# First layer of a graph network: for 66 blocks, one tile of rows is formed on TensorE instead of gathered; x waits in DRAM between the layers

## The chip, the core and the metric

The kernel runs on one core of a Trainium2 chip. The metric is the device time of one execution in microseconds (us); lower is better. A core has five engines with an instruction queue each: TensorE (PE in the profile; its weight loads are shown as PEld), VectorE (DVE), ScalarE (ACT), GpSimd (POOL) and SyncE (SP, which here only issues DMAs). TensorE writes its results to PSUM, a small accumulator memory of eight banks; the other working memory is SBUF.

## The reference

A graph of 6250 nodes with 128 features and 200,000 edges, sorted by destination. Two layers, each with a layer norm and a ReLU in front and the input added back:

```python
h = relu(layernorm(x))                      # layer 1: attention, 8 heads of 16
z = (h @ W).reshape(N, 8, 16)
el, er = einsum(z, attn_l), einsum(z, attn_r)
e = leaky_relu(el[src] + er[dst], 0.2)
a = exp(e - segment_max(e, dst)[dst])
out = segment_sum(z[src] * a, dst) / segment_sum(a, dst) + bias
x = x + out
h = relu(layernorm(x))                      # layer 2: messages with edge attributes
s, v = (h[:, :32] @ W_up_s), (h[:, 32:] by W_up_v)
tpw = silu(silu(edge_attr_8 @ A1 + b1) @ A2 + b2) @ A3
message = segment_sum(products of s[src], v[src], edge_attr_4, tpw, dst) / 10
x = x + (message by W_out_s, W_out_v)
```

Each layer thus needs, for each edge, the row of a table of nodes that `src` names: 136 numbers in layer 1 (128 features and 8 values of `el`), 128 in layer 2.

## The kernel before

Edges go in tiles of 128 (one edge to a partition): 1563 tiles. Sixteen tiles make a block, 98 blocks; the kernel first checks that the destinations of a block lie in a window of 128 nodes that moves on by 64 from block to block, and then runs `even_edges`.

**Set-up.** `tile_even_edges` computes the table of layer 1 (`t0`, in DRAM, `ft` in the profile) and starts the gathers of block 0 into `z_first`.

**Gathers.** `gather` (L830) issues one indirect DMA for each tile from GpSimd (L832): 128 indices from a column of `src_col` (`fsrc`), 128 rows of the table into one of the 16 columns of a tile `g`. `z_pool` holds five such tiles. `take_rows(g + 3)` is called at the head of iteration g of the block loop; GpSimd runs ahead of it as far as free `g` tiles allow, since nothing else is in its queue.

**Layer 1.** The loop `for g in range(NG - 3)` (L1288) is software pipelined and written out by hand, PE, DVE and ACT in the order of the text: iteration g does `logits` and `maxima` for block g, `neighbours`, `weights`, `weighted` and `sums` for block g - 1, and the destination side (`masks_of`, `turned`, `er_of`, `er_sum`) for block g + 1, and makes 0/1 matrices from the destinations (`ends_of`, which calls `one_hot`, L1043) for block g + 2. `logits` (L1112) is the first to read the gathered rows of block g: it starts an iteration. `sums` (L1171) is the weighted sum over the edges as matmuls, 16 tiles of float32, each as two matmul instructions, and the last reader of a `g` tile. `ended` adds up the windows; after every second block `node_x` to `node_s` do what follows for 128 nodes: x plus bias from `with_bias` (L1175), the sums divided, added to x, layer norm, `wup`, and the rows of the table of layer 2 (`t1`, also `ft` in the profile) to DRAM. x stays in `x_all` (`fx_all`), 25 KB in each partition of SBUF, from there to the end of layer 2. In PSUM the node step has a bank `p_n`, the others are `p_u`, `p_m`, `p_d` (two), `p_er` and `pe` (two).

**Layer 2.** The same gathers of 128 numbers from `t1`, a small network for each edge on TensorE (`network`, `tensor_weights`), products on VectorE (`messages`, L1458 to L1467), sums on TensorE (`sums1`, L1475), and `node1`, which adds to `x_all` and stores.

Of the kernel before, what the change touches and what calls it, by code (L numbers as in the profile page):

```python
# [9 lines left out]
F32 = mybir.dt.float32  # L10
BF = mybir.dt.bfloat16
I32 = mybir.dt.int32
AF = mybir.ActivationFunctionType
OP = mybir.AluOpType
# [4 lines left out]
P = 128  # L19
# [3 lines left out]
ZW = F + H  # L23
# [6 lines left out]
KB = 16  # L30
# [933 lines left out]
def even_edges(tc, v):  # L964
# [7 lines left out]
    with ExitStack() as ctx:  # L972
        const = ctx.enter_context(tc.tile_pool(name="fconst", bufs=1))
        z_pool = ctx.enter_context(tc.tile_pool(name="fz", bufs=5))

        def gathered(table, tiles, width):
            return gather(z_pool.tile([P, KB, ZW], F32, name="g"), table, tiles, width)
# [4 lines left out]
        nc.sync.dma_start(jp, nums[:, NB * KB + TG + P :])  # L982
        rsel = const.tile([P, P // KB, P], BF, name="frsel")
        nc.sync.dma_start(rsel, v["rsel"])
        x_all = const.tile([P, NX, P], F32, name="fx_all")
        bias_b = const.tile([P, F], F32, name="fbias_b")
        nc.sync.dma_start(bias_b, bias.to_broadcast([P, F]))
        wup = const.tile([P, P], F32, name="fwup")
# [70 lines left out]
            return carry, agg  # L1059


        in_order = {mybir.EngineType.PE, mybir.EngineType.DVE, mybir.EngineType.Activation}
        with tc.manual_schedule(engines=in_order), \
                tc.tile_pool(name="l0", bufs=2) as l0, \
                tc.tile_pool(name="l0n", bufs=2) as l0n, \
                tc.tile_pool(name="l0_ps", bufs=1, space=PSUM) as l0_ps:


            def ends_of(c, q):
# [103 lines left out]


            def with_bias(i, n):  # L1175
                x_i = x_all[:, i : i + n, :]
                nc.sync.dma_start(x_i, xp[i * P : (i + n) * P].rearrange("(j p) f -> p j f", p=P))
                nc.vector.tensor_add(x_i, x_i, bias_b[:, None, :].to_broadcast([P, n, F]))

            def node_x(u):  # L1180
                i, n, agg = u["i"], u["n"], u["agg"]
                x_i = x_all[:, i : i + n, :]
                if n == 1:
                    with_bias(i, n)
                rd = l0n.tile([P, 2, H], F32, name="rd")[:, :n]
                nc.vector.tensor_scalar(rd, agg[:, :n, F:ZW], 1e-9, None, op0=OP.max)
                nc.vector.reciprocal(rd, rd)
                sums_ = agg[:, :n, :F]
                heads = sums_.rearrange("p j (h d) -> p j h d", d=D)
                nc.vector.tensor_mul(heads, heads, rd.unsqueeze(3).to_broadcast([P, n, H, D]))  # L1190
                nc.vector.tensor_add(x_i, x_i, sums_)
                u["mv"] = moments(l0n, x_i, n, f"n{n}")

            def node_d(u):
# [2 lines left out]
            def node_h(u):  # L1197
                i, n = u["i"], u["n"]
                rs, mr = normal(l0n, u["mv"], u["rs"], n, f"n{n}")
                xn = u["xn"] = l0n.tile([P, 2, P], F32, name="xn")  # L1200
                nc.scalar.activation(xn[:, 0, :], x_all[:, i, :], AF.Identity, bias=mr[:, 0, :],
                                     scale=rs[:, 0, :])
                if n == 2:
                    nc.vector.tensor_scalar(xn[:, 1, :], x_all[:, i + 1, :], u["mv"][:, 1, 0:1],
                                            rs[:, 1, :], op0=OP.subtract, op1=OP.mult)

            def node_t(u):
                n = u["n"]
                p_n = l0_ps.tile([P, 512], F32, name="p_n")
                p_n = u["p_n"] = p_n.rearrange("p (j f) -> p j f", f=P)  # L1210
                for j in range(n):
                    nc.tensor.transpose(p_n[:, j, :], u["xn"][:, j, :], ident)
                h_t = u["h_t"] = l0n.tile([P, 2, P], F32, name="h_t")
                nc.scalar.activation(h_t[:, :n], p_n[:, :n], AF.Relu)

            def node_s(u):
                i, n, p_n = u["i"], u["n"], u["p_n"]
                for j in range(n):
                    nc.tensor.matmul(p_n[:, 2 + j, :], u["h_t"][:, j, :], wup, start=True, stop=True)
                sv = l0n.tile([P, 2, P], F32, name="sv")  # L1220
                nc.scalar.activation(sv[:, :n], p_n[:, 2 : 2 + n], AF.Copy, scale=PRE)
                first = i * P - W0
                if i == 0:
                    nc.sync.dma_start(t1[: P - W0, :], sv[W0:, 0, :])
                else:
                    nc.sync.dma_start(t1[first : first + n * P].rearrange("(j p) f -> p j f", p=P),
                                      sv[:, :n])
# [13 lines left out]
            def take_rows(g):  # L1241
                if 0 < g < NG:
                    c = cs[g]
                    t = c["b"] * KB + c["o"]
                    c["z"] = gathered(t0, range(t, t + c["kt"]), ZW)

            def bank_of(c, bank="p_u"):
                if c["o"] == 0:
# [39 lines left out]
            for g in range(NG - 3):  # L1288
                take_rows(g + 3)
                c, b4 = cs[g], (cs[g - 1] if g else None)  # L1290
                n1 = cs[g + 1] if g + 1 < NG else none
                n2 = cs[g + 2] if g + 2 < NG else none
                nodes = []
                logits(c)
                ends_of(n2, 0)
                if n1 is not none:
                    masks_of(n1)
                turned(n1, 0)
                maxima(c)
                ends_of(n2, 1)  # L1300
                if b4:
                    neighbours(b4, cs[g - 2] if g > 1 else None, c)
                    if g > 1:
                        nodes = ended(cs[g - 2], st)
                turned(n1, 1)
                er_of(n1, 0)
                if b4:
                    weights(b4)
                for n in nodes:
                    node_x(n)  # L1310
                er_of(n1, 1)
                turned(n1, 2)
                if b4:
                    bank_of(b4)
                    weighted(b4, 0)
                turned(n1, 3)
                er_of(n1, 2)
                if b4:
                    weighted(b4, 8)
                for n in nodes:  # L1320
                    node_d(n)
                    node_h(n)
                ends_of(n2, 2)
                er_of(n1, 3)
                if b4:
                    sums(b4, 0)
                for n in nodes:
                    node_t(n)
                if n1 is not none:
                    er_sum(n1)  # L1330
                ends_of(n2, 3)
                for n in nodes:
                    node_s(n)
                if b4:
                    sums(b4, 8)
                if g == NG - 4:
                    for q in range(4):
                        ends_of(c1, q)
                    masks_of(c1)
                    for q in range(4):  # L1340
                        turned(c1, q)
                        er_of(c1, q)
                    er_sum(c1)
            with_bias(NX - 2, 2)

            logits(c3)
            masks_of(c2)
# [49 lines left out]
        with tc.manual_schedule(engines=in_order), \  # L1397
# [72 lines left out]
            def sums1(u):  # L1470
# [3 lines left out]
                for k in range(m):  # L1474
                    nc.tensor.matmul(blk[b]["p_u"][:, :MW], u["s"][:, k, :], u["mj"][:, k, :],  # L1475
                                     start=k0 + k == 0, stop=k0 + k == KT[b] - 1)

            def node1(i, agg):
                x_i = x_all[:, i, :]
                p_n = l1_ps.tile([P, 4, P], F32, name="p_n", bufs=1)  # L1480
                for q in range(2):
                    nc.tensor.transpose(p_n[:, q, :], agg[:, q * P : (q + 1) * P], ident)
                m_t = l1n.tile([P, 2, P], F32, name="m_t")
                nc.scalar.copy(m_t, p_n[:, :2])
                for q in range(2):
                    nc.tensor.matmul(p_n[:, 2, :], m_t[:, q, :], wout[:, q, :], start=q == 0, stop=q == 1)
                nc.vector.scalar_tensor_tensor(x_i, p_n[:, 2, :], POST, x_i, op0=OP.mult, op1=OP.add)
                if i == 0:
                    nc.sync.dma_start(out[: P - W0, :], x_all[W0:, 0, :])
                else:  # L1490
                    nc.sync.dma_start(out[i * P - W0 : (i + 1) * P - W0, :], x_i)

# [18 lines left out]
                network(0, step)  # L1511
            tensor_weights(us[0])
            us[0]["s"] = one_hot(0, us[0]["m"], iota_p)
            ready, done = [], []
            carry = agg = None
            ends = None
            for i, u in enumerate(us):
                b, k0, m = u["b"], u["k0"], u["m"]
                if k0 == 0:
                    take_rows(b + 2)  # L1520
                if b + 1 < NB:
                    network(b + 1, k0 // 4)
                if i + 1 < NU:
# [32 lines left out]
            for j in range(2):  # L1556
                for q in range(2):
                    nc.tensor.matmul(p_o[:, j, :], m_t[:, 2 * j + q, :], wout[:, q, :],  # L1558
                                     start=q == 0, stop=q == 1)
            x_i = x_all[:, NX - 2 :, :]  # L1560
            nc.vector.scalar_tensor_tensor(x_i, p_o[:, :2], POST, x_i, op0=OP.mult, op1=OP.add)  # L1561
            nc.sync.dma_start(out[first:].rearrange("(j p) f -> p j f", p=P), x_i)

# [137 lines left out]
```

## Time and profile before

| | |
|---|---|
| time, median of 3 runs | 5254.23 us (5251.97 to 5270.86) |
| the profiled execution's own time | 4015.26 us |
| its span | 4013.5 us |
| granted TensorE clock, mean | 0.809 |
| layer 1, roughly | 93 to 2045 us of the span |
| layer 2, roughly | 2045 to 4008 us |

The profiled execution is 1239 us shorter than the median of the timed runs. No view of the profile shows what the timed runs have more.

The busy share of an engine is that of its instructions over the span; issuing a DMA from SP and waiting are not counted. In the second part of the page the span is cut into 40 slices, and a digit is a share in tenths; PEclk is the clock that the chip granted TensorE in tenths of the full one. In a row of a group of instructions stand the line, the engine, the operation, output and input, how often, the busy us and the mean ns of one, and after the second bar the idle time of the engine just before them and what ended it ("issue": nothing that the profile shows). The stretches give, for each, its length and the busy time of PE, PEld, DVE, ACT and POOL, each with its number of instructions, then the granted clock, the share of the DMA engines and GB/s.

### The profile page before, as it was taken

How to read it: one execution, taken by the hardware profiler on the slowest of the kernel's cores; microseconds unless marked ns; L12 is line 12 of the kernel's file. 1: busy time of each engine (PE TensorE's matmuls, PEld its weight loads, DVE VectorE, ACT ScalarE, POOL GpSimd, SP SyncE). 2: the span in 40 equal slices, each digit the busy share in tenths (PEclk: the TensorE clock that was granted, in tenths of full speed). 3: DMA queues.
4: the chain of work that ended last, by engine and by line, in shares of the span. 5: the costliest groups of instructions: out<-in, count | busy, mean ns of one | idle time of the engine just before them, and what ended most of it. 6: DMA issues, size and time to landing. Idle time of an engine off the chain costs nothing. (4 is left out here: it accounts for less than half of the span.)

```text
span 4013.5 us, 45637 instructions
## 1 busy us (share of the span) xinstructions
PE 2837.4 (71%) x14592; PEld 2369.6 (59%) x14592; DVE 2191.8 (55%) x5376; ACT 1374.3 (34%) x3450; POOL 2993.5 (75%) x3158
## 2 busy tenths in 40 slices
PE   3666666666666666666677777777787777787787
PEld 3665655565556555555665665565666555666565
DVE  4544444444444444444456666666666666666666
ACT  3322222222222222222333434344434343443443
POOL 6777777777777777777757777777777777777776
PEclk6666666666666666666679999999999999999999
DMA  7222222222222222222212222222222222222221
GB/s 206 57 57 58 57 58 57 58 57 58 57 58 57 58 58 58 57 58 57 58 48 60 60 59 61 59 60 59 60 60 60 59 61 59 60 59 60 60 60 51
DMA packets 174105, 248.25 MB, mean 62 GB/s; under 512 B 70944, under 2 KB 123072, under 8 KB 173856
## 3 DMA queue, kind: packets, MB, share of 16 engines
q0 software_dynamic: 100032, 211.47, 19.7%
q1 hardware_dynamic: 73536, 33.70, 3.1%
q8 instruction: 118, 1.93, 0.2%
q14 instruction: 131, 1.07, 0.1%
q10 hardware_dynamic: 288, 0.07, 0.0%
HBM read 234.73 MB, written 9.99 MB: 61 GB/s over the span
## 5 line engine op out<-in xcount | busy, mean ns | idle before, releaser
L832 POOL DMA_INDIRECT g<-ft,fsrc x3110 | 2959.7, 952 | 975.4 <-issue 892.3
L1475 PE MATMUL p_u<-mj,s 128*128 128x256 f32 x3126 | 802.8, 401 | 354.7 <-DVE mj L1467 354.0
L1475 PEld LDWEIGHTS p_u<-mj,s 128*128 128x128 f32 x3126 | 582.8, 195 | 547.3 <-DVE mj L1467 478.2
L1171 PE MATMUL p_u<-g,s 128*128 128x136 f32 x3062 | 581.8, 369 | 0.5 <-DVE g L1166 0.5
L1171 PEld LDWEIGHTS p_u<-g,s 128*128 128x128 f32 x3062 | 557.2, 273 | 0.6 <-DVE g L1166 0.6
L1458 DVE TENSOR_TENSOR vy<-g,p_i 128x384 f32<-128x384 f32 x391 | 216.5, 554 | 596.3 <-DMA g<-ft,fsrc 569.3
L1442 ACT ACTIVATE p_w<-p_w,yb 128x64 f32<-128x64 f32 x1563 | 450.3, 288 | 113.6 <-PE p_w L1438 73.5
L1112 DVE TENSOR_TENSOR e_s<-g,er 128x128 f32<-128x128 f32 (+1 forms) x98 | 28.4, 290 | 749.3 <-DMA g<-ft,fsrc 749.2
L1438 PE MATMUL p_w<-fa3p,h 128*128 128x256 f32 x1564 | 403.8, 381 | 0.0
L1088 PE MATMUL p_d<-fident,s 128*128 128x128 f32 x1563 | 392.8, 418 | 5.1 <-DVE s L1043 5.1
L1116 PE MATMUL pe<-fident,e_s 128*128 128x128 f32 x98 | 39.7, 406 | 454.0 <-DVE e_s L1113 454.0
L1438 PEld LDWEIGHTS p_w<-fa3p,h 128*128 128x128 f32 x1564 | 285.7, 193 | 120.9 <-issue 57.4
L1081 ACT COPY mk<-p_m 128x385 f32<-128x385 f32 (+1 forms) x99 | 47.6, 481 | 903.1 <-PE p_m L1078 903.1
L1088 PEld LDWEIGHTS p_d<-fident,s 128*128 128x128 f32 x1563 | 318.9, 229 | 43.6 <-DVE s L1043 31.6
L1423 ACT ACTIVATE h<-p_h,fb 128x512 f32<-128x512 f32 x196 | 134.7, 687 | 561.9 <-PE p_h L1421 561.9
L1090 ACT CAST d<-p_d 128x512 bf16<-128x512 f32 x391 | 228.5, 585 | 201.3 <-PE p_d L1088 153.5
L1166 DVE TENSOR_TENSOR g<-g,pe 128x1024 f32<-128x1024 f32 x193 | 225.4, 1208 | 127.8 <-ACT g L1157 125.2
L1116 PEld LDWEIGHTS pe<-fident,e_s 128*128 128x128 f32 x98 | 16.6, 169 | 470.6 <-issue 462.6
L1043 DVE TENSOR_TENSOR s<-p_i,fdloc 128x512 f32<-128x512 f32 x391 | 266.2, 681 | 14.5 <-ACT p_i L1417 14.5
L1043 DVE TENSOR_TENSOR s<-fiota,fdloc 128x512 f32<-128x512 f32 x391 | 265.6, 681 | 5.9 <-ACT fmasks L1036 5.8
L1428 ACT ACTIVATE h<-p_h,fb 128x512 f32<-128x512 f32 x196 | 134.7, 687 | 362.0 <-PE p_h L1425 362.0
L1462 DVE TENSOR_REDUCE vd<-vy 128x128 f32<-128x384 f32 x391 | 228.9, 585 | 0.0
(172 smaller groups left out, 3417.5 us busy)
## 6 DMA issues: line engine op xcount, KB each, us to landing
g<-ft,fsrc POOLq DMA_INDIRECT x3110, 2.5
ft<-in_e_f_dram SPq DMA_DIRECT2D x98, 64.0 KB
yb<-in_e_y_dram SPq DMA_DIRECT2D x98, 32.0 KB
fx_all<-in_e_xp_dram SPq DMA_DIRECT2D x48, 64.0 KB
ft<-sv SPq DMA_DIRECT2D x47, 64.0 KB
out_dram<-fx_all SPq DMA_DIRECT2D x47, 64.0 KB
ft<-zt SPq DMA_DIRECT2D x6, 408.0 KB
fxs<-in_e_xp_dram SPq DMA_DIRECT2D x6, 384.0 KB
```

Of the source, the lines that this page charges most:

```text
L832: nc.gpsimd.indirect_dma_start(out=to[:, k, :width], out_offset=None, in_=table, in_offset=bass.IndirectOffsetOnAxis(ap=src_col[:, t : t + ...
L1043: nc.vector.tensor_tensor(s[:, :m], iota[:, None, :].to_broadcast([P, m, P]), dloc[:, t : t + m].unsqueeze(2).to_broadcast([P, m, P]), OP. ...
L1088: nc.tensor.transpose(p_d[:, k, :], c["s"][q][:, k, :], ident)
L1090: nc.scalar.copy(d[:, :m], p_d[:, :m])
L1166: nc.vector.tensor_mul(zh, zh, p_a[:, k0 : k0 + m].unsqueeze(3).to_broadcast([P, m, H, D]))
L1171: nc.tensor.matmul(c["p_u"][:, :ZW], c["s"][k // 4][:, k % 4, :], c["z"][:, k, :], start=c["o"] + k == 0, stop=c["o"] + k == KT[c["b"]] - 1)
L1423: nc.scalar.activation(c["h1"], p_h, AF.Silu, bias=b1)
L1438: nc.tensor.matmul(w[:, k : k + n].rearrange("p k a u -> p (k a u)"), c["h2"][q // 4][:, q % 4, :], a3p[:, :n].rearrange("p k f -> p (k f) ...
L1442: nc.scalar.activation(w[:, k, ::2, :], w[:, k, ::2, :], AF.Copy, scale=c["yb"][:, k0 + k, 0:1])
L1458: nc.vector.tensor_mul(vy, v_n, y_p)
L1462: nc.vector.tensor_reduce(vd, vy.rearrange("p t i u -> p t u i"), AX.X, OP.add)
L1475: nc.tensor.matmul(blk[b]["p_u"][:, :MW], u["s"][:, k, :], u["mj"][:, k, :], start=k0 + k == 0, stop=k0 + k == KT[b] - 1)
```

## The change

In 66 blocks of layer 1 (`dense`: blocks 6 to 93 but those divisible by four) the sixteenth tile is no longer gathered. Its 128 rows come from TensorE as 0/1 matrix times table. The table, 50 tiles of 128 nodes, is held in SBUF as three bfloat16 parts that add up to the float32 value (`t0s`, 40 KB in each partition); `split` reads it back from DRAM, three tiles at a time, five times in each of the iterations 0 to 2 and twice in iteration 3. The 50 tiles are treated as three thirds of 17, 17 and 16. For a dense block `spread` turns the 128 source numbers (less their third's start) by one float32 matmul into a row that every partition holds, in the free quarter of the bank `pe`; `ends_to` compares it with the node numbers of each of the 17 positions (two VectorE instructions of 1152 and 1024 elements, output bfloat16, into the memory of `z_first`, which is free by then); `rows_of` multiplies each of the 17 0/1 matrices with the three parts of the up to three tiles at that position at once: 51 matmuls of 408 (three of them 272) columns, summed in the bank `p_n`; `taken` selects the third that the edge's source is in and writes column 15 of the `g` tile. The 51 matmuls of block b are put at six places in the iterations b - 2 (27 of them) and b - 1 (24). The node step gives up `p_n` and uses the end of `p_u`.

To make room `x_all` goes: `node_x` takes x in a tile of its own and stores it to a DRAM tile `x1`; layer 2 reads it back for each 128 nodes (`node_rows`) when their first block starts.

```diff
+        x1 = dram.tile([NX, P, P], F32, name="fx1")
-        x_all = const.tile([P, NX, P], F32, name="fx_all")
+        NR = -(-NX // 3)
+        dense = {b for b in range(6, NB - 4) if b % 4}
...
+            ND = NB - 1
+            key = l0d.tile([P, ND], F32, name="key")
+            nc.vector.tensor_scalar(key, src_col[:, KB - 1 : ND * KB : KB], float(W0), None, op0=OP.add)
+            part = l0d.tile([P, ND, 3], F32, name="part")
...
+            order = sorted(range(NR), key=lambda k: (k > 0, 2 * NR + k < NX, k))
+            half = (NR + 1) // 2
+            place = l0d.tile([P, NR], F32, name="place")
+            for j, k in enumerate(order):
+                nc.vector.tensor_scalar(place[:, j : j + 1], jp[:, 0:1], -1.0, float(P * k),
+                                        op0=OP.mult, op1=OP.add)
+            t0s = l0d.tile([P, 3, NX, ZW], BF, name="t0s")
+            def split(i, n):
+                zr = l0.tile([P, 3, ZW], F32, name="zr")[:, :n]
...
+                    nc.sync.dma_start(zr, rest.rearrange("(j p) f -> p j f", p=P))
+                r = l0.tile([P, 3, ZW], F32, name="zr2")[:, :n]
+                nc.scalar.copy(t0s[:, 0, i : i + n, :], zr)
+                nc.vector.tensor_sub(r, zr, t0s[:, 0, i : i + n, :])
+                nc.scalar.copy(t0s[:, 1, i : i + n, :], r)
+                nc.vector.tensor_sub(t0s[:, 2, i : i + n, :], r, t0s[:, 1, i : i + n, :])
+            def spread(c):
+                b = c["b"]
+                nc.tensor.matmul(c["at"]["pe"][:, 3 * P :], key[:, b : b + 1].to_broadcast([P, P]), ident,
+                                 start=True, stop=True)
+            def ends_to(c, h):
+                n = half if h == 0 else NR - half
+                oh = c["oh", h] = ohs[:, h * half : (h + 1) * half, :]
+                nc.vector.tensor_tensor(
+                    oh[:, :n], c["at"]["pe"][:, 3 * P :].unsqueeze(1).to_broadcast([P, n, P]),
+                    place[:, h * half : h * half + n].unsqueeze(2).to_broadcast([P, n, P]), OP.is_equal)
+            def rows_of(c, k0, n):
+                if k0 == 0:
+                    p_x = l0_ps.tile([P, 512], F32, name="p_n")
+                    c["p_x"] = p_x[:, : 3 * ZW].rearrange("p (r f) -> p r f", f=ZW)
+                for k in range(k0, min(k0 + n, NR)):
+                    i = order[k]
+                    m = len(range(i, NX, NR))
+                    for s in range(3):
+                        nc.tensor.matmul(c["p_x"][:, :m, :], c["oh", k // half][:, k % half, :],
+                                         t0s[:, s, i::NR, :], start=k == 0 and s == 0,
+                                         stop=k == NR - 1 and s == 2)
+            def taken(c):
+                b, z = c["b"], c["z"][:, KB - 1, :]
+                nc.vector.tensor_scalar(z, c["p_x"][:, 0, :], part[:, b, 0:1], None, op0=OP.mult)
+                for r in (1, 2):
+                    nc.vector.scalar_tensor_tensor(z, c["p_x"][:, r, :], part[:, b, r : r + 1], z,
+                                                   op0=OP.mult, op1=OP.add)
             def with_bias(i, n):
-                x_i = x_all[:, i : i + n, :]
+                x_i = l0n.tile([P, n, P], F32, name=f"x{n}", bufs=3 - n)
...
             def node_x(u):
                 nc.vector.tensor_add(x_i, x_i, sums_)
+                nc.sync.dma_start(x1[i : i + n].rearrange("j p f -> p j f"), x_i)
...
             def node_t(u):
-                p_n = l0_ps.tile([P, 512], F32, name="p_n")
+                if "bank" in u:
+                    p_n = u["bank"][:, 2 * P :]
...
             def take_rows(g):
-                    c["z"] = gathered(t0, range(t, t + c["kt"]), ZW)
+                    c["z"] = gathered(t0, range(t, t + c["kt"] - (c["b"] in dense)), ZW)
...
                 logits(c)
+                if to: spread(n2)
                 ends_of(n2, 0); masks_of(n1); turned(n1, 0); maxima(c)
+                if to: ends_to(n2, 0)
+                if at: rows_of(n1, half, 4)
                 ends_of(n2, 1); neighbours(b4, ...); turned(n1, 1); er_of(n1, 0)
+                if at: rows_of(n1, half + 4, NR)
                 weights(b4)
+                if at: taken(n1)
                 node_x; er_of(n1, 1); turned(n1, 2); weighted(b4, 0)
+                if to: ends_to(n2, 1)
                 turned(n1, 3); er_of(n1, 2); weighted(b4, 8)
+                if to: rows_of(n2, 0, 3)
                 node_d, node_h; ends_of(n2, 2); er_of(n1, 3); sums(b4, 0)
-                node_t
+                if to: rows_of(n2, 3, 3)
                 er_sum(n1); ends_of(n2, 3)
-                node_s; sums(b4, 8)
+                sums(b4, 8); node_t
+                if to: rows_of(n2, 6, half - 6)
+                node_s
+                for i in range(g * 15, min(g * 15 + 15, NX), 3):
+                    split(i, min(3, NX - i))
...
+            def node_rows(i, n=1):
+                x_i = l1n.tile([P, n, P], F32, name=f"x{n}", bufs=3 if n == 1 else 1)
+                nc.sync.dma_start(x_i, x1[i : i + n].rearrange("j p f -> p j f"))
+                return x_i
...
                 if k0 == 0:
                     take_rows(b + 2)
+                    if b % 2 == 0:
+                        xs[b // 2] = node_rows(b // 2, 1 if b < NB - 2 else 2)
```

The loop of layer 1 stands here shortened, several calls to a line (`to`: block g + 2 is dense; `at`: block g + 1 is); the lines with a plus are new, and `node_t` and `node_s` have moved behind the second half of `sums`.

## The prediction

> **What bounds the kernel now.** I read the page first, for the engine that never rests.
>
> ```profile
> PE 2837.4 (71%) x14592; PEld 2369.6 (59%) x14592; DVE 2191.8 (55%) x5376; ACT 1374.3 (34%) x3450; POOL 2993.5 (75%) x3158
> ...
> POOL 6777777777777777777757777777777777777776
> PEclk6666666666666666666679999999999999999999
> ...
> L832 POOL DMA_INDIRECT g<-ft,fsrc x3110 | 2959.7, 952 | 975.4 <-issue 892.3
> ```
>
> 75% does not look like a bound, but the row of the gathers shows what the other 25% are: 0.3 us of "issue" before each, a wait for nothing. So I took the groups of the even middle of layer 1 (200 to 2000 us of the span).
>
> ```profile
> L832 POOL DMA_INDIRECT g<-ft,fsrc x1426 | 1365.6, 958 | 434.6 <-issue 405.9 <-PE p_u L1171 11.3 <-DMA g<-ft,fsrc 8.2
> ...
> L1112 DVE TENSOR_TENSOR e_s<-g,er 128x128 f32<-128x128 f32 x89 | 26.0, 292 | 719.5 <-DMA g<-ft,fsrc 719.5
> ```
>
> A gather costs (1365.6 + 434.6) / 1426 = **1.262 us** of GpSimd, and 3126 of them 3945 of the 4013.5 us. The second row says the same from the other side: VectorE waits for the rows at the head of every block, 719.5 / 89 = 8.1 us. In the order of time one block starts at 996.48 and the next at 1016.74: 20.2 us, 16 gathers. The other waits of GpSimd are one of 27.9 us between the layers and pieces of 0.3 us.
>
> The engine that gets the work is TensorE, and its clock decides what it can take. These are the order of time on PE, twice the same 16 matmuls in one block, and stretches of 1 us in the block before.
>
> ```profile
> 1025.75 3.97 PE L1171 MATMUL p_u<-g,s 128*128 128x136 f32 x16
> ...
> 1030.52 2.02 PE L1171 MATMUL p_u<-g,s 128*128 128x136 f32 x16
> ```
>
> ```profile
> 1006.00:1007.00 1.00, 0.43 (x10) 0.33 (x9) 1.00 (x2) 0.58 (x1) 0.69 (x2) 0.50 0.10 26
> ...
> 1012.00:1013.00 1.00, 1.00 (x9) 1.00 (x8) 0.00 (x0) 0.00 (x0) 0.69 (x2) 0.73 0.17 44
> 1013.00:1014.00 1.00, 0.60 (x6) 0.40 (x4) 0.00 (x0) 0.00 (x0) 0.73 (x1) 1.00 0.27 70
> ...
> 1016.00:1017.00 1.00, 0.00 (x0) 0.00 (x0) 0.27 (x1) 0.00 (x0) 0.70 (x2) 0.50 0.11 30
> ```
>
> The clock is 0.50 or 1.00, nothing between: it rises after about 5.5 us without a gap (1006.9 to 1012.4) and falls after about 2.4 us of rest. In layer 2, where PE pauses for 1.3 us at most places, it stays at 1.00. The 0.6 of the page is a mean of the two. What a block costs at the full clock stands at the start of layer 1, where PE was late and worked through:
>
> ```profile
> 116.64 0.27 PE L1116 MATMUL pe<-fident,e_s 128*128 128x128 f32 x1
> 116.75 0.33 PE L1078 MATMUL p_m<-fmasks,frsel 128*128 128x385 bf16 x1
> ...
> 122.30 3.95 PE L1171 MATMUL p_u<-g,s 128*128 128x136 f32 x32
> ...
> 128.75 0.53 PE L1078 MATMUL p_m<-fmasks,frsel 128*128 128x385 bf16 x1
> ```
>
> From 116.64 to 126.25 is **9.6 us**, waits included, against 17.1 us (996.48 to 1013.60) for the same work mostly at half clock.
>
> **What goes.** 66 gathers x 1.262 = 83.3 us of GpSimd. Next in line is TensorE. Three dense blocks and one other take GpSimd 61 x 1.262 = 77.0 us, against 80.8 before.
>
> **What PE gets.** No row has a bf16 matmul of 408 columns in a stream. The nearest is the one of 385 columns above: 0.53 us at half clock, 0.33 at full, so the part that goes with the clock is 0.20 us at full clock, 0.21 for 408 columns. From below, page "TensorE: Matmul & The Clock Gate" of the Trainium skill (Part 2, Back-to-back issue gap) prices a stream at N/2.4 ns, an estimate of 0.17 us; float32 rows fit it (256 columns in 0.236 us, 8 in 1.89 us at 3000.97, at two passes each). I take 0.20: 51 x 0.20 = 10.2 us, and 0.2 for `spread` (four passes like it, L1088, took 0.60 us warm for four instructions, it has two). The node step adds some 0.5 us every second block. Four blocks: 4 x 9.9 + 3 x 10.4 = **70.8 us, 6.2 below GpSimd's 77.0** (66.3 at 0.17, 72.3 at 0.21). It is a little better than that, since the 9.6 us hold 2 us of waits for ACT and the new matmuls lie in them.
>
> Here a rule of that page speaks against the change: in Part 3 (What overlaps and what doesn't) it lets a weight load run beside a matmul only if they use different rows of the array, and all these use all 128. At its P/1.2 ns a load would add 0.107 us to each matmul: 51 x (0.17 + 0.107) + 0.2 = 14.3 us, four blocks 39.6 + 42.9 = 82.5 us, 1.7 more than before, or +37 us over 22 such fours. The rows say otherwise: 128 columns with a load each take 0.131 us (8 in 1.05 us, L1421 at 3002.70), 256 columns 0.236; twice the columns cost 1.8 times, which leaves 0.03 us for everything that does not grow with them. I follow the rows. The sum stands up to (77.0 - 39.6) / 3 = 12.5 us or 0.24 us a matmul; at 0.27 the gain is gone.
>
> **Will the clock stay up?** Nearly all gaps inside a block (2.25 us at 1001.4, 0.6 and 0.6 later) are where the new matmuls stand, so a dense block is one busy stretch of 17 to 19 us. The two lighter iterations of each four rest 3 to 5 us; the next then runs some 5.5 us at half clock, which costs under 3 us each. 70.8 + 2 x 3 = 76.8: no room left, but a cold PE has no rests and so turns warm, and up to two blocks of lag lie in the five `g` tiles: in the block above `sums` ends 17 us after the rows landed, and GpSimd needs the tile some 60 us after.
>
> **The rest, at nothing.** `ends_to`: 1152 + 1024 elements at the rate of L1166 (1024 in 1.21 us) 2.6 us, `taken` 3 x 0.29 (L1265, 136 from PSUM); 3.4 us for VectorE, which is busy 44% of 20.2 = 8.9 us: 12.3 of 18.9. In its queue `taken` waits for the last of the 24 matmuls, which PE does before it turns the weights; behind it stand `weighted` and all of `node_x`, which wait for that turn anyway; uncovered, 1 us per dense block, within the lag. `split`: 17 times two ACT copies (about 0.5 us, L1081) and two subtractions (0.57 us, L953), with two buffers some 8 to 10 us at the end of iterations 0 to 2; the last row-wait at the start is 7.7 us per block already from 147.92, so the lag is worked off; if not, once up to 20 us. The 25 small set-up instructions on VectorE (about 4 us) stand before 67.94, where it idles 18.4 us for `fq_i`. x: 49 loads go from the head of SP's queue to places two node steps ahead (40 us for a landing of 3), the stores and reloads are 6.3 MB more on DMA engines that are 22% busy. On SP the reload for node block i + 3 waits for the store of i to land, some 3 us, and the loads of `ft` and `yb` stand behind it; they have three buffers, 40 us. At the end of layer 1 the store of x stands before the last store to `t1`, on which the 27.9 us wait between the layers hangs: **+1 us**, the only one I charge (0 to 3).
>
> **The sum.** -83.3 + 1 = -82.3 us on the profiled execution's 4015.26: 3933, its span 3931. The timed runs are 1239 us longer and no view says where. If GpSimd's gathers are slower there (1239 / 3126 = 0.40 us each), the saving grows with the time: 82.3 x 5254.23 / 4015.26 = 107.7, **5146.5 us**. If it is fixed, 5172. I take the first, since GpSimd is what sets the time from end to end.
>
> **Rivals.**
> - *PE at half clock.* It decides from 0.27 us a matmul; at half clock one costs 0.34 to 0.42. Four blocks then take 4 x (17.1 - 2.5) + 3 x (17.5 to 21.6) = 111 to 123 us against 80.8: 22 x (30 to 42) = +660 to +930 us, 5910 or more. For it: 0.66 in layer 1 now, and the unexplained 1239 us, which would fit a PE that is cold in the timed runs. Against: the clock rows. 9%.
> - *Weights not hidden*, or other gaps that eat the room (PE late by 12.5 to 14.5 us a block): -0.5 to +1%, about 5254 to 5290. 11%.
> - *GpSimd held up by the new VectorE work*: if a gather stood still for all 3.4 us, +224 - 83 = +141 us, 5395. Against: a gather takes 958 ns where VectorE is busy 44%, 944 in layer 2 where it is 66%. 4%.
> - *The gather's place is taken by another wait*, such as the start's 20 us and the SP queue: 5190 to 5254. 5%.
> - *The forecast*, 5120 to 5200: 71%.
>
> A measurement of this kernel tells 0.5% (26 us) from no change. Faster 0.74, same 0.07, slower 0.19. The range for eight in ten runs from 5120 (a PE that relieves the DMAs) over the forecast's own end at 5200 to 5300, where the small losses lie.
>
> **What would show it.** Right: 3060 gathers at 1.26 us with "issue" before them, `e_s` still waiting for `g`, blocks of 18.9 us, a granted clock near 0.9 in layer 1, L1141 at 0.17 to 0.21 us in its stream. Wrong: gathers waiting for `p_u`, or `e_s` for PE; a clock of 0.5 in dense blocks; a longer gap between the layers.

## The result and the profile after: 5827.07 us, slower by 10.8%

| | before | after |
|---|---|---|
| median of 4 runs | 5256.6 us (5251.97 to 5270.86) | 5827.07 us (5819.8 to 5830.49) |
| ratio, 95% interval | | 1.1078 (1.1054 to 1.1103) |
| the profiled execution | 4015.26 us, span 4013.5 | 5827.96 us, span 5826.2 |
| granted clock of the profiled execution | 0.809 | 0.767 |
| a block of layer 1 / of layer 2 in its trace (mean of blocks 10 to 90) | 20.2 / 20.0 us | 30.3 / 28.0 us |

The forecast was 5146.5 us. The profile of after agrees with its timed runs; that of before does not. Each set of runs is made on one chip, with runs of before beside it, and the sets fall into two groups: in the **late sets** the median of before is 5246 to 5259 us, in the **prompt sets** 4015 to 4020. All the timed runs above were late; the profiled execution of before was prompt. Why a set is late or prompt stays open. Of the sets below, that of k1 and k2 is late and that of m1, eight minutes later, is prompt, and both bear the chip number 9; if that number names one chip, the chip alone does not decide it.

Lines of the page of after: engines, the clock in 40 slices, the gathers, and `taken`, the reader of the new rows.

```profile
PE 3476.7 (60%) x18090; PEld 2636.6 (45%) x18090; DVE 2438.5 (42%) x5765; ACT 1378.5 (24%) x3484; POOL 2936.7 (50%) x3092
...
PEclk6677777777777777777776788878878888887878
...
L832 POOL DMA_INDIRECT g<-ft,fsrc x3044 | 2902.8, 954 | 2783.3 <-issue 876.9
...
L1147 DVE TENSOR_SCALAR g<-p_n,part 128x136 f32<-128x136 f32 x66 | 23.7, 359 | 726.4 <-remote 698.5
```

No engine is busy above 60%. A gather still costs 0.954 + 0.30 us, but the idle time ahead of the gathers is 2783.3 us instead of 975.4. The view of waits says for whom GpSimd stood (us in total, times, longest):

```profile
POOL g L832 <- DVE mj L1577: 772.0, 92, 17.0
POOL g L832 <- PE p_n L1141: 382.5, 29, 14.2
POOL g L832 <- ACT h_t L1301: 288.2, 33, 14.2
```

It waits for free `g` tiles, in layer 1 and in layer 2, whose code for TensorE has not changed. `taken` waits 726.4 / 66 = 11.0 us each time, mostly for "remote": nothing that the trace can name. The order of time in one dense block shows what that is:

```profile
1527.23 2.23 PE L1141 MATMUL p_n<-t0s,fz_first 128*128 128x408 bf16 x12
...
1539.27 0.36 DVE L1147 TENSOR_SCALAR g<-p_n,part 128x136 f32<-128x136 f32 x1 [11.11 <-remote]
1539.30 0.27 ACT L1241 COPY g<-pe 128x128 f32<-128x128 f32 x1 [8.43 <-remote]
...
1552.44 0.95 POOL L832 DMA_INDIRECT g<-ft,fsrc  x1 [11.73 <-PE p_m L1162]
```

The last of the 51 matmuls is recorded as done at 1529.5, its reader is let go at 1539.27, and ScalarE, which waits for a transpose recorded at 1530.92, at 1539.30. TensorE's results come 8 to 10 us after their recorded ends; an end of a matmul is modelled in these traces, so the row can look done before the result is there. So I add up, for each trace, the time from the recorded end of a TensorE result to the start of its reader on VectorE or ScalarE, as far as that engine stood idle (above 0.2 us). These sums of **late results** are some 2040 us in layer 1 of after (two engines often wait for one delay) and 1440 in layer 2, against 22 and at most 16 in the profiled execution of before.

### The profile page after: what moved, and what is told of

It is laid out like the page before. It is cut to its first block, busy times and chain, and to the rows that moved or that the text cites. A ratio compares the mean times of both kernels' runs of the same rounds, so it can differ in the third digit from the quotient of the medians.

```text
span 5826.2 us, 53276 instructions
## 1 busy us (share of the span) xinstructions
PE 3476.7 (60%) x18090; PEld 2636.6 (45%) x18090; DVE 2438.5 (42%) x5765; ACT 1378.5 (24%) x3484; POOL 2936.7 (50%) x3092
## 3 DMA queue, kind: packets, MB, share of 16 engines
q0 software_dynamic: 97920, 206.87, 13.1%
## 4 chain that ended last, share of the span: by engine, by line
PE 23%; another core or an unknown queue 18%; issue 8%; ACT 6%; DVE 5%; DMA 0%; POOL 0%; DVEq 0%; ACTq 0%
PE p_u L1585 9%; ACT p_w L1552 4%; PE p_w L1548 3%; PE p_h L1531 2%; PE p_n L1141 2%; PE p_u L1255 2%; PE p_h L1535 1%; DVE vd L1572 1%; DVE vy L1568 1%; DVE mj L1577 1%; ACT h L1538 1%; DVE mj L1574 1%; PE p_n L1597 1%; PE p_n L1601 0%
## 5 line engine op out<-in xcount | busy, mean ns | idle before, releaser
L832 POOL DMA_INDIRECT g<-ft,fsrc x3044 | 2902.8, 954 | 2783.3 <-issue 876.9
L1585 PE MATMUL p_u<-mj,s 128*128 128x256 f32 x3126 | 935.9, 452 | 397.5 <-DVE mj L1576 146.3
L1585 PEld LDWEIGHTS p_u<-mj,s 128*128 128x128 f32 x3126 | 683.0, 227 | 607.3 <-DVE mj L1577 210.2
L1141 PE MATMUL p_n<-t0s,fz_first 128*128 128x408 bf16 (+1 forms) x3366 | 752.8, 372 | 113.0 <-issue 111.6
L1183 PEld LDWEIGHTS <-d 128*128 128x128 bf16 x1563 | 99.2, 109 | 980.6 <-ACT d L1174 883.1
L1141 PEld LDWEIGHTS <-fz_first 128*128 128x128 bf16 x3366 | 346.3, 106 | 388.4 <-issue 214.2
L1535 PE MATMUL p_h<-h,fa2p 128*128 128x512 f32 x392 | 248.2, 720 | 233.9 <-ACT h L1533 226.1
L1533 ACT ACTIVATE h<-p_h,fb 128x512 f32<-128x512 f32 x196 | 134.7, 687 | 1043.4 <-remote 435.3
L1147 DVE TENSOR_SCALAR g<-p_n,part 128x136 f32<-128x136 f32 x66 | 23.7, 359 | 726.4 <-remote 698.5
L1570 DVE TENSOR_TENSOR p_w<-g,p_w 128x128 f32<-128x128 f32 x391 | 114.5, 293 | 426.9 <-ACT p_w L1552 332.2
L1601 PE MATMUL p_n<-fwout,m_t 128*128 128x128 f32 x192 | 57.7, 455 | 378.1 <-issue 266.0
```

Source lines behind the costliest of these rows:

```text
L832: nc.gpsimd.indirect_dma_start(out=to[:, k, :width], out_offset=None, in_=table, in_offset=bass.IndirectOffsetOnAxis(ap=src_col[:, t : t + ...
L1141: nc.tensor.matmul(c["p_x"][:, :m, :], c["oh", k // half][:, k % half, :], t0s[:, s, i::NR, :], start=k == 0 and s == 0, stop=k == NR - 1 ...
L1183: nc.tensor.matmul(c["p_er"][:, 4 * q + k].rearrange("p s h -> p (s h)"), c["d", q][:, k, :], er_w, start=True, stop=True)
L1533: nc.scalar.activation(c["h1"], p_h, AF.Silu, bias=b1)
L1535: nc.tensor.matmul(p_h.rearrange("p q e -> p (q e)"), a2p, c["h1"].rearrange("p q e -> p (q e)"), start=True, stop=True)
```

## The experiments

**Is it the change, or the set? Before once more, and the parts of the change (a late set, before 5245.84 us).** `e1_before` is unchanged. `e2_x_only` has `dense = set()` and no `split`. `e3_one_part` multiplies one of the three bf16 parts. `e4_no_rows` leaves the 66 gathers out and forms nothing (VectorE copies the rows of the tile beside):

```diff
-dense = {b for b in range(6, NB - 4) if b % 4}        # e2
+dense = set()
-                    for s in range(3):                # e3
+                    for s in range(1):
-                nc.vector.tensor_scalar(z, c["p_x"]...)   # e4; no spread, ends_to, rows_of, split
+                nc.vector.tensor_copy(c["z"][:, KB - 1, :], c["z"][:, KB - 2, :])
```

> The kernel before, unchanged, with a new profile. In the profile of the changed kernel, TensorE's results reach VectorE and ScalarE 4 to 14 us after the matmuls' recorded ends, in layer 2 too, where nothing of TensorE's work was changed. Theory A (the added matmuls of layer 1 cause this): before has none of it, whatever its time; profile near 4015 us. Theory B (most executions of any version are in a condition in which TensorE's results come late, and the one profiled execution of before was not): this profile takes about 5254 us and shows such late results in both layers, about 6 us for each of the 196 blocks. Theory C (x in DRAM slows the layers): as A.

> Only the move of x to DRAM: no block is dense, all rows are gathered, nothing is split. Theory A: as before, within 0.5% (5254 us). Theory B: as before too. Theory C: slower by a good part of the 570 us, mostly in layer 2, where each reload waits for a store.

> The changed kernel with the first of the three bf16 parts alone (17 matmuls for a dense block, not 51; the rows are rounded to bf16). Theory A with the cost by the number of matmuls: a third of the loss, about 5254 + 0.33 x 570 = 5440 us or less, since part of it then fits beside the gathers. If the loss comes from the VectorE parts, from split or from x: about 5827 as with three parts. If 17 matmuls fit wholly: 5150 to 5254.

> The 66 gathers are left out and nothing forms their rows: VectorE copies the rows of tile 14 to tile 15 in these blocks (wrong edges there); no split, x in DRAM. It gives the worth of 66 gathers alone. If GpSimd's gathers pace the timed runs as they pace before's profiled one: 5254 - 83 to 5254 - 108, so 5146 to 5172 us. If something else paces the timed runs (theory B with TensorE the bound): less than 30 us gained.

| | median, us | ratio to before, 95% interval | block of layer 1 / 2, us |
|---|---|---|---|
| e1_before | 5244.41 | 0.9991 (0.9976 to 1.0005) | 24.0 / 28.0 |
| e2_x_only | 5247.72 | 1.0002 (0.9985 to 1.0018) | 24.1 / 27.8 |
| e3_one_part | 5366.09 | 1.0200 (1.0155 to 1.0246) | 25.3 / 27.9 |
| e4_no_rows | 5159.55 | 0.9820 (0.9782 to 0.9859) | 23.1 / 28.0 |

The new profile of before has a span of 5255.3 us. From its page, and from the waits of GpSimd (us in total, times, longest):

```profile
L832 POOL DMA_INDIRECT g<-ft,fsrc x3110 | 2985.8, 960 | 2130.2 <-issue 878.8
...
POOL g L832 <- DVE mj L1467: 763.0, 91, 17.0
POOL g L832 <- ACT mk L1081: 304.8, 85, 4.2
```

The gather is what it was, 0.96 + 0.30 us. Of the 1242 us between the two profiles of before, 2130.2 - 975.4 = 1155 lie in the rests of GpSimd, and the results of TensorE are late by some 1160 us in layer 1 and 1430 in layer 2. Theory B holds for the lateness, and theory A falls as its cause: it is there without the change, and layer 2 of after (28.0 us a block) is as slow as that of before (28.0). Theory C falls: with x in DRAM the time is that of before within 0.2% (e2). What the change adds lies in layer 1 alone, and e3 and e4 give its terms: 66 gathers are worth 5247.7 - 5159.6 = 88 us, 1.34 each, give or take 20 by the interval of e4 alone; 83.3 were forecast. The rows of one part cost (5366.1 - 5159.6) / 66 = 3.1 us a block. That is 0.18 for each of 17 matmuls if nothing else costs, but `spread`, `split`, `ends_to` and `taken` are in it too. The other 34 matmuls, which e3 leaves out and nothing else, cost (1.1078 x 5245.8 - 5366.1) / 66 / 34 = 0.20 us each, a little more than one takes in its stream (0.17). **The added matmuls are paid in full**, some 10 us a block, for 1.3 saved.

The order of time of e1, in one block of layer 1, shows why there is no room for them:

```profile
1705.38 0.37 PE L1088 MATMUL p_d<-fident,s 128*128 128x128 f32 x1 [1.13 <-issue]
1705.39 0.18 PEld L1088 LDWEIGHTS p_d<-fident,s 128*128 128x128 f32 x1 [0.53 <-issue]
1705.81 0.94 POOL L832 DMA_INDIRECT g<-ft,fsrc  x1 [0.30 <-issue]
1706.78 0.37 PE L1088 MATMUL p_d<-fident,s 128*128 128x128 f32 x1 [1.02 <-issue]
...
1709.87 0.56 PE L1137 MATMUL pe<-mx,fshift 128*128 128x1 f32 x2
...
1710.83 0.96 POOL L832 DMA_INDIRECT g<-ft,fsrc  x1 [4.08 <-ACT mk L1081]
```

TensorE crawls: its instructions start 0.70 or 1.40 us apart with "issue" before them (four transposes took 0.67 us at 1731.65). In layer 1 of e1, from 200 us on, 92 of its matmuls start 1.385 to 1.425 us after the one before; in the profiled execution of before none does. The granted clock has little to do with it: it was 1.00 over 45 of these steps and 0.50 over 35.

At 1706.75 the gathers stop, for want of a free tile; at 1709.7, 3 us later, TensorE is quick again. I counted the starts of matmuls around the stops of over 1.5 us in layer 1. In e1 (88 stops) there are 0.6 in the third us after the last gather's end and 4.9 in the fifth. In after (89 stops) there are 0.3 to 0.7 in each of the seven us before that end and the three after it, then 4.4, while the gathers stay away for 11.1 us; from the thirteenth us after they resume there is less than one again. So in layer 1 gathers and TensorE take turns: 16 x 1.26 and a rest of 3.9 us make the 24.0 us of a block, and in after, 15.25 x 1.26 and a rest of 11.1 us make the 30.3. In layer 2 of e1 the same count shows no such step (2.3 in the us before a stop, 1.4 to 2.4 in the eight after it).

Slower DMA packets are not the reason for the crawl. In layer 1 those that bring instructions take as long in e1 as in the profiled execution of before (median 0.99 us on queue q8 in both), and so do those of the gathers (mean 0.135 and 0.136 us).

**Is it the gathers that slow TensorE?** `f4_half` gathers 8 tiles of a block of layer 1, `h2_quarter` 4, and VectorE copies their rows to the others. `f1_rest8` and `f2_rest4` make GpSimd wait for a landing after every eighth or fourth gather. `f3_22_blocks` has 22 dense blocks. The set of f1 to f4 turned out prompt (before 4015.13), so f1 (as `h1_rest8`) and h2 were run in a later, late one (before 5258.54).

```diff
-    c["z"] = gathered(t0, range(t, t + c["kt"]), ZW)
+    c["z"] = gathered(t0, range(t, t + min(4, c["kt"])), ZW)      # h2; 8 in f4
+            if k % 8 == 7:                                        # f1; 4 and 3 in f2
+                nc.gpsimd.tensor_copy(breath, to[:1, k, :1])
-        dense = {b for b in range(6, NB - 4) if b % 4}            # f3
+        dense = {b for b in range(6, NB - 4) if b % 4 == 2}
```

> The kernel before with a rest in GpSimd's queue after every eighth gather: GpSimd copies one number of the rows just asked for, so it waits for their landing, about 1.2 us, with the copy 1.6 to 2 us. Theory G (TensorE crawls, one instruction in about 0.7 us, once some 8 gathers have gone out without a rest, until 2 to 3 us after they stop): the crawl goes away or gets shorter; the matmuls' results come on time; a block is 20.2 + 2 x 1.8 = 23.8 us in both layers, so layer 1 as before (24.0), layer 2 from 27.5 to about 24: 5250 - 340 = about 4900 us. Theory P (TensorE is held up by its own work, whatever GpSimd does): the results come as late as before; with the rests on GpSimd the time is 5250 or more.

> The changed kernel with 22 dense blocks (every fourth) in place of 66. Theory G (TensorE's added work is paid in full, since GpSimd stands still while TensorE finishes): the cost is 1/3 of the 570 us, 5245 + 22 x 8.7 = about 5436 us. Rival (three dense blocks in four leave no slack, one in four would be hidden by the other three): 5217 to 5245 us, no loss.

> The kernel before with only the first 8 tiles of each block of layer 1 gathered; VectorE copies their rows to the other 8 (so the rows of half the edges are wrong there), TensorE's work is unchanged. Theory G: runs of 8 gathers, then a rest until the next tile of rows is free; TensorE's results are on time in layer 1 and a block there takes some 12 to 17 us (24.0 before): 4100 to 4600 us in all. Theory P: results as late as before in layer 1, a block 20 us or more, about 4900 us or more.

> The kernel before with only the first 4 tiles of each block of layer 1 gathered; VectorE copies their rows to the other 12 (three quarters of the edges get wrong rows), TensorE's work is unchanged. On a chip where before takes 5250 us: Theory G: no late results in layer 1, a block there takes 12 to 14 us (12.6 with 8 gathers on the other chip) against 24.0; 4000 to 4250 us in all, with layer 2 as slow as before. Theory P: late results in layer 1 as before, a block 20 us or more. On the other chip it shows what bounds layer 1 without gathers: 12 to 13 us a block, about 3250 us in all.

Prompt set: f1 4467.23 us (1.1128, 1.1106 to 1.1151), f2 4492.36 (1.1191), f3 4008.57 (0.9985, 0.9977 to 0.9994; twice more the same ratio), f4 3320.26 (0.8271), in another prompt set 3308.5. None has late results, so they say nothing of theory G. But f1 shows that there the rests of GpSimd are paid: 313 us of waits for a landing and 83 of copies stand in a loss of 452.

Late set: h1 takes 5233.67 us (0.9959, 0.9912 to 1.0007), the crawls stay (results late by some 1160 and 1430 us), and its forecast missed. But it does not do what was meant. The trace shows one waiting rest a block, of 1.7 us after the sixteenth gather, where two were meant, and it falls into the stop that GpSimd makes there anyway (3.6 us on average, 3.9 in e1). The copy after the eighth gather does not wait. Whether a short rest would be enough, the first part of theory G, is thus not tested.

h2 takes 4182.36 us (0.7951, 0.7925 to 0.7978), and its layer 1 has 13.2 us a block with results late by 48 us in all, while its layer 2, unchanged, has 27.9 and 1420. The same copy on ScalarE in layer 1 of e1 (200 to 2300 us), of h2 (200 to 1300) and of the profiled execution of before (200 to 2000), idle time after the second bar:

```profile
L1081 ACT COPY mk<-p_m 128x385 f32<-128x385 f32 x87 | 41.9, 481 | 932.4 <-PE pe L1137 494.6 <-remote 335.1 <-PE pe L1131 33.3
```

```profile
L1081 ACT COPY mk<-p_m 128x385 f32<-128x385 f32 x83 | 39.9, 481 | 353.7 <-PE p_m L1078 353.7
```

```profile
L1081 ACT COPY mk<-p_m 128x385 f32<-128x385 f32 x89 | 42.9, 482 | 850.8 <-PE p_m L1078 850.8
```

What tells is who ends the wait, not its length (9.6 us each in the last row, where blocks wait for rows). In h2 and in the prompt execution it is always the matmul that makes `p_m`. In e1 it is, for 863 of the 932.4 us, a later matmul or nothing that the trace can name: the result came late. TensorE's work is the same in all three. Theory P falls for layer 1: there **the gathers slow TensorE**, not its own work. In layer 2 no run leaves gathers out, so for its lateness this stays an inference.

**Their asking or their landing? And less work for TensorE (a late set, before 5251.77).** `k2_plain_dma` gathers 4 tiles and brings the other 12 by one DMA from SP; `k1_bf16_turn` halves the passes of the 16 transposes of `turned`.

```diff
+    nc.sync.dma_start(c["z"][:, 4 : c["kt"], :ZW], t0[r0 : r0 + (c["kt"] - 4) * P, :]...)   # k2
-    nc.tensor.transpose(p_d[:, k, :], c["s"][q][:, k, :], ident)                            # k1
+    nc.tensor.transpose(p_d[:, k, :], high[:, k, :], identb)     # high: upper halves, as bf16
```

> The kernel before with less work for TensorE and everything else as it is: the 16 transposes of 0/1 matrices of a block of layer 1 read the upper halves of the float32 numbers as bf16, one pass in place of two (0.109 us each at full clock, so 0.87 us a block less). Theory S (on the chips where TensorE's results come late, GpSimd and TensorE take turns in layer 1, so TensorE's work counts in full there): 98 x 0.87 = 85 us less, 5250 to about 5165. On the chips where GpSimd never waits: 4015, no change. If TensorE's work is hidden behind the gathers on both: no change on either.

> The kernel before with 4 tiles of each block of layer 1 gathered by GpSimd and the other 12 brought by one plain DMA from SP (12 x 128 whole rows of the table, not those the edges name, so their results are wrong): the same bytes into the same tile, without GpSimd's work for them. On a chip where before takes 5250: if GpSimd's asking for gathers is what slows TensorE (theory G1): as with 4 gathers and VectorE copies, results on time in layer 1, a block 12 to 14 us, about 4180 us in all. If the landing of so many rows in SBUF is (theory G2): results late in layer 1, a block 20 us or more, 4800 us or more. On the other chip: 12 to 14 us a block, 3250 us or so.

k2 takes 4178.63 us (0.7959), layer 1 at 13.1 us a block with results late by 49 us, and the same copy is always let go by its own matmul:

```profile
L1081 ACT COPY mk<-p_m 128x385 f32<-128x385 f32 x84 | 40.5, 482 | 355.4 <-PE p_m L1078 355.4
```

The same bytes land in the same tile, and there is no crawl. So it is GpSimd's gathers, not the landing of rows (G1). One difference is left: k2 reads rows that stand side by side, a gather reads scattered ones, and no run separates that from GpSimd's asking. k1 is **slower**, 5414.95 us (1.0321, 1.0292 to 1.0351): GpSimd's rests grow from 3.9 to 6.0 us a block, the late results at `h_t` from 252 to 560 us. So theory S falls as it was put. Less time on TensorE does not as such save any; that it also counts which of its instructions fall into a crawl is only argued.

**Columns or number? The change in a prompt set.** `m1_narrow` multiplies one of the up to three tiles of a position, 136 columns in place of 408.

```diff
-                    m = len(range(i, NX, NR))
+                    m = 1
```

> The changed kernel again. The runs beside it show which kind of chip it is on: in one kind the kernel before takes 5250 us and TensorE's results come late (A and B of the profiles: 5255 and 5826 us), in the other 4015 us and they come on time. On the first kind: 5827 us again. On the second: the forecast's own sum is 4015 - 82 = 3933 us; from the run with 22 dense blocks (-6.5 us there, of which 22 x 1.262 = 27.8 were saved and 22 given back by gathers that last 15 ns longer each): 4015 - 83 + 66 = about 3998 us, if TensorE keeps up at three dense blocks in four; 4050 us or more if it does not.

> The changed kernel with the 51 matmuls of a dense block a third as wide: only the tile of the first third is multiplied, 136 columns in place of 408 (rows whose source is in another third are wrong). Number of instructions, waits and VectorE's work are as in the changed kernel. On a chip where before takes 5250 us and the change 5827: if the loss goes with the columns (TensorE's time at its recorded rate, about 0.06 us a matmul): a third, about 5160 + 66 x 51 x 0.065 = 5380 us. If it goes with the number of instructions: about 5827. On a chip where before takes 4015: 3950 to 3970, as the changed kernel (3966).

Both runs of m1 (3956.79 and 3953.08 us; 0.9839 and 0.9841) and the two repeats of f3 fell into prompt sets, so what is paid in a late set, the columns or the number of the matmuls, stays open. `g1_after`, the changed kernel itself, takes **3966.31 us there against 4020.07: 0.9864 (0.9847 to 0.9880), faster by 54 us**. From its page:

```profile
PEclk6698998898889888988689999999999999999999
...
L832 POOL DMA_INDIRECT g<-ft,fsrc x3044 | 2931.7, 963 | 955.6 <-issue 871.4
...
L1141 PE MATMUL p_n<-t0s,fz_first 128*128 128x408 bf16 (+1 forms) x3366 | 670.8, 350 | 0.0
```

and from its order of time:

```profile
1006.22 0.68 DVE L1044 TENSOR_TENSOR s<-fiota,fdloc 128x512 f32<-128x512 f32 x1
1006.35 1.36 POOL L832 DMA_INDIRECT g<-ft,fsrc  x1 [0.30 <-PE p_u L1255]
1007.04 1.42 PEld L1141 LDWEIGHTS <-fz_first 128*128 128x128 bf16 x9
1007.15 1.72 PE L1141 MATMUL p_n<-t0s,fz_first 128*128 128x408 bf16 x9
```

GpSimd rests 0.3 us before a gather and no longer, as in the first profile, and the clock stays up. But a gather of layer 1 comes every 1.288 us, not 1.263 (200 to 1900 us): 183 gathers (97 before) last over 1.05 us, like the one at 1006.35, and 158 of the 183 run beside a `one_hot` of VectorE. Of 66 x 1.262 = 83 us saved, 1497 x (0.9836 - 0.9598) = 36 go back, since that is the mean length of a gather after and before. It is not the new work of VectorE that they stand beside: of 196 gathers that overlap an `ends_to`, 3 last that long. Beside a `one_hot`, which both kernels have, a gather takes 1.064 us in the mean, 0.991 before. Why that grew is not shown.

## Why the prediction was wrong

- **What bounds the kernel.** Right for the profiled execution, wrong for the runs that are timed. There (e1) GpSimd stands some 90 times in layer 1 for 3.9 us, because TensorE is late with the tile that it needs.
- **The step that failed** is the last of the sum: "If GpSimd's gathers are slower there (1239 / 3126 = 0.40 us each), the saving grows with the time", taken because "GpSimd is what sets the time from end to end". e1 shows gathers of the same 1.26 us. The surplus is TensorE's lateness, 3.8 us a block in layer 1 and 8.0 in layer 2 (98 x 11.8 = 1156 of the 1239 us). With it the room of 6.2 us for four blocks is gone, and 10 us of matmuls a block are paid in full. No factor on the saving could have held that, and a fixed saving (5172) would have missed as well.
- **What goes**: 83.3 us said; 88 measured, give or take 20 (e2 to e4). Right.
- **What TensorE gets**: 0.20 us a matmul said. In g1 nine take 1.72 us, (1.72 - 0.34) / 8 = 0.173, with the loads beside them (1.42 us for nine). The rule of the Trainium skill that was weighed ("TensorE: Matmul & The Clock Gate", Part 3, What overlaps and what doesn't), by which a load here would not be hidden, an estimate of 0.277 us a matmul, does not hold in these traces. The estimate from below, N/2.4 ns or 0.17, does; but Part 2 of that page (Back-to-back issue gap) gives this formula for an isolated matmul and puts a stream of large ones at less, so "prices a stream" reads it too freely. Right, then, and in a late set worth nothing: the recorded rate is the same in after (12 in 2.23 us), the result is 10 us late.
- **The clock**: near 0.9 in layer 1 said; 0.89 in g1 (200 to 1900 us), 0.75 in after (200 to 2900). In layer 1 of e1 it is 0.64, in that of the profiled execution of before 0.65, so there it does not tell late from prompt. (In layer 2 it is 0.80 and 0.98; what the clock itself costs there is not separated.) The "5.5 us" and "2.4 us" are the reading of one block: over layer 1 of the trace of before nine of ten rises came 3.0 to 6.2 us after TensorE took up work, and the falls follow no one length of rest.
- **At nothing.** x in DRAM: right (e2). The wait between the layers: 28.1 us for 27.9 in g1. `split`: GpSimd loses nothing in g1, and waits once for 59.5 us in after. The VectorE work: `ends_to` takes 2 x 1.275 us in g1 (2.6 said), and no gather waits for it. What the sum for the prompt condition lacks are the 36 us by which the gathers last longer: 4015 - 82 + 36 = 3969, and g1 takes 3966. The rival "GpSimd held up by the new VectorE work" (+224 us, 4%) is not borne out as put: the long gathers stand beside VectorE's `one_hot`, not beside the new work.
- **The rivals.** "PE at half clock" gave 5910 or more at 9% and named "the unexplained 1239 us, which would fit a PE that is cold in the timed runs". It looked at the right engine: TensorE is slow in the timed runs. But in layer 1 not by its clock: that is the same in e1 as in the prompt execution, streams are recorded at the full rate, and the results come late. That 5827 lies near its 5910 is luck. Of the signs named, "gathers waiting for `p_u`, or `e_s` for PE" came nearest; they wait for `p_n`, `p_d` and for what follows from them.

No version here beats both kernels in a late set with every row in place: e2 and h1 are level with before, e4, h2 and k2 are faster but leave rows out, and k1 is slower.

## What to carry to other kernels

Where a profiled execution is 24% shorter than the timed runs, as here, it can be of another condition, and no sum on it holds until the surplus has an engine: profile again, and compare the waits of each engine, not its busy time. Work moved to an engine "with room" needs that room in the condition that is timed. And look for results that reach their reader late: the row of the producer then looks quick and idle, and only the reader's wait shows the price.

## What the hardware showed that was not expected

- In layer 1 of the late sets TensorE starts one instruction in 0.70 us, or one in 1.40, once a run of GpSimd's gathers has lasted some 10 us, at a granted clock of 1.00 as of 0.50, and is quick again 3 to 4 us after they stop (0.6 starts a us, then over 4). With 4 gathers a block (h2), and with 12 tiles by plain DMA (k2), results are late by 48 and 49 us in place of 1160. What the steps of 0.70 us come from is not explained.
- Two kinds of sets, 5250 and 4017 us for the same kernel, 31% apart; the change is 10.8% slower in one and 1.4% faster in the other.
- A change that takes passes away from TensorE's transposes cost 3.2% in a late set (k1).
- A gather beside a `one_hot` of VectorE can last 1.36 us, not 0.94 (158 of 424 such gathers in g1 last over 1.05 us, 25 of the 1058 others).
